# Two reorderings on VectorE around the seven-product multiplications of a fused two-layer attention kernel

## The chip, the cores and the metric

The kernel runs on one core of one Trainium2 chip. The metric is the time of one execution on the device, in microseconds; less is better. A profile of one execution of the kernel before is at hand, with a trace of every instruction of each engine.

## The reference: what is computed

Two layers run over 32 independent batches of 512 nodes with 512 features, in fp32.

```python
# layer 0, eight heads of 64 columns
q, k, v = x @ Wq.T + bq, x @ Wk.T + bk, x @ Wv.T + bv
logits = q @ k.T / sqrt(64) + log(clip(adj, 1e-8))       # per head
out    = softmax(logits) @ v                             # heads joined
y      = layer_norm(x + out @ Wo.T + bo) * gamma + beta
# layer 1
f      = y @ fc_w.T + fc_b
lg     = (f @ q_w.T + q_b) + (f @ k_w.T + k_b).T
m      = lg + (1 - adj) * -1e9
att    = softmax(where(m >= 0, m, 0.01 * m))
result = att @ f + y
```

The log of the adjacency is applied in the kernel as a factor on the exponentials, and layer 1 is computed as `(att @ n) @ fc` plus a residual, where `n` holds the normalised rows before gamma and beta.

## The kernel before, in words

The program is written out by hand: every engine gets its instructions in the order in which the Python code issues them, and a tile framework adds the semaphore waits that the data need. TensorE (PE in the profile) does the matrix products, VectorE (DVE) and ScalarE (ACT) the elementwise work, and the SyncE queue (SP) issues all transfers.

**Slots.** For each batch `b` there are four slots `slot(b, p)`, one for each pair of heads. A slot computes the scores and exponentials of its pair (`score`, lines L849 to L858), multiplies the exponentials by the adjacency (`factors`, L866), and forms the values of the pair before (`values`, L891). Into this are woven the stages of earlier and later batches, so that several batches are in work at once. `factors(b, p, 0)` handles the first two of the four 128x1024 blocks of exponentials, and `factors(b, p, 1)` the other two.

**Products with seven multiplications.** Large products are done by a Strassen-Winograd scheme: seven products of quarters in place of eight, at the price of sums and differences of quarters on VectorE. Every product is 16 matmuls of 128x64 weights by 256 columns, recorded at L213 (the helper `halves`).

**First slot of batch b, for b from 2 to 31 (30 slots).** Besides its own pair it does the following.

- `scale(b - 1, 0)` (L946) multiplies two head outputs by the inverse row sums `R`, and `first_difference` (L954) prepares a quarter for the later output projection. Then comes `factors(b, 0, 0)`.
- `eT(b - 2)` (L572): four transposes in 32x32 blocks of `eP`, the layer-1 attention weights of batch b - 2. Sixteen transfers `eP<-L` have moved the blocks to their places.
- `seven_z(b - 2)`: the product of the normalised rows `n` with those weights. Its quarters are called A (of `n`) and E (of `eP`). `before0` makes `t1 = E12 - E11` (L1048, in a free half of a tile named `R`) and `s1 = A21 + A22` (L1049, in a tile named `third`); `before1` makes A21 = A11 - A21 (L1052); `after0` overwrites E11 and A11 (L1055, L1056). `unit0` runs mul(1), which reads the old A11 and E11, and mul(5), which reads `s1` and `t1`; `unit1` runs mul(6), which reads the new A11 and E11, and mul(2); `unit2` and `unit3` run mul(7), mul(3) and mul(4).
- `scaled(b - 2, ...)` (L464): the residual `yb = n * gamma`, in two halves of 128x1024. `new_yb` takes the buffer `yb`, of which there is one.
- `divided(b - 1, 2)` inverts the sums of the last two pairs of batch b - 1 and sends them through DRAM to `R` (transfers `d<-c`, then `R<-d`).

**Second slot of batch b (b from 1 to 31).** `scale(b - 1, 2)` (L946) waits for that `R`; `first_sum` (L961) adds quarters of the head outputs. Then come `factors(b, 1, 0)` and `sums`, a 128x1024 sum (L876), `factors(b, 1, 1)`, and the output projection `seven_wo` of batch b - 1: mul(1), then mul(5), which reads the result of `first_sum` (matmuls `<-wo_s,oT`), then subtractions of quarters (L770) ahead of its own mul(6).

The order of the work around the change is the order of these calls. The transfers that feed `eP` are issued in the fourth slot of the batch before, after the transfers `R<-d` and eight of the adjacency (`cT`).

Of the kernel before, what the change touches and what calls it, by code (L numbers as in the profile page):

```python
# [30 lines left out]
def kernel(  # L31
# [58 lines left out]
    NC = N // P  # L90
# [4 lines left out]
    KH = DC // 2  # L95
# [114 lines left out]
    def halves(to, left, right, start, stop):  # L210

        for h in range(2):
            nc.tensor.matmul(  # L213
                to[ts(h, DK)], left[:, ts(h, DK)], right,
                start=start, stop=stop, skip_group_check=True,
            )
# [95 lines left out]
    def transpose_units(src, dst, psum, evict, name):  # L312

        units = []
        for i in range(4):
            def unit(i=i):
                pt = psum.tile([P, 512], FP, tag="m", name=f"pt_{name}_{i}")
                for c in range(4):
                    nc.tensor.transpose(pt[:, ts(c, P)], src[:, c, ts(i, P)], ident)
                evict(dst[:, i, :], pt)  # L320
            units.append(unit)
        return units
# [137 lines left out]
    def over(row, cs):  # L460
        return row.unsqueeze(1).to_broadcast([P, cs.stop - cs.start, D])

    def scaled(s, cs):
        nc.vector.tensor_mul(s["yb"][:, cs, :], s["n"][:, cs, :], over(K["gamma"], cs))  # L464
# [39 lines left out]
    def fast(ctx):  # L504
# [8 lines left out]
        S = [dict() for _ in range(B)]  # L513
# [56 lines left out]
        def transposes(dst, src):  # L570
            return [
                lambda c=c: nc.vector.transpose(dst[:, c, :], src[:, c, :]) for c in range(4)  # L572
            ]
# [251 lines left out]
        def long_banks(b):  # L825
            return lambda: [
                lone[i].rearrange("p (n f) -> p n f", n=KH) for i in (2, 0, 1)
            ]
# [32 lines left out]
        def factors(b, p, half):  # L861

            s = S[b]
            for kc in (2 * half, 2 * half + 1):
                at = s["at", p, kc]
                nc.vector.scalar_tensor_tensor(  # L866
                    at, cT[:, kc, :].unsqueeze(1).to_broadcast([P, 2, N]), ADJ_MIN, at,
                    ALU.max, ALU.mult,
                )
# [72 lines left out]
        def scale(b, p):  # L942
            s = S[b]
            for k in range(2):
                oT = s["oT"][p + k]
                nc.vector.tensor_mul(oT, oT, s["R", p][:, k, :])  # L946

        def first_difference(b, to=None):

            s = S[b]  # L950
            oT = s["oT"]
            s["s3"] = to or act.tile([P, KH, H], FP, tag="oT", name=f"s3_{b}", bufs=6)
            for c in range(KH):
                nc.vector.tensor_sub(s["s3"][:, c, :], oT[c][:, :H], oT[c][:, H:])  # L954

        def first_sum(b, to=None):

            oT = S[b]["oT"]
            for c in range(KH):
                into = oT[c][:, H:] if to is None else to[:, c, :]  # L960
                nc.vector.tensor_add(into, oT[c][:, H:], oT[KH + c][:, H:])  # L961
# [39 lines left out]
        def seven_z(b):  # L1001


            s = S[b]
            n, e = s["n"], s["eP"]
            s["zT"] = zT = L1
            s1 = third
            t1 = S[b + 1]["R", 2][:, 1, :].rearrange("p (c n) -> p c n", c=KH)
            A = {f"{i + 1}{j + 1}": n[:, ts(j, KH), ts(i, H)] for i in range(2) for j in range(2)}
            E = {f"{i + 1}{j + 1}": e[:, ts(j, KH), ts(i, H)] for i in range(2) for j in range(2)}  # L1010
            C = {f"{i + 1}{j + 1}": zT[:, ts(i, KH), ts(j, H)] for i in range(2) for j in range(2)}
            left = {1: A["11"], 2: A["12"], 3: A["12"], 4: A["22"], 5: s1, 6: A["11"], 7: A["21"]}
            right = {1: E["11"], 2: E["21"], 3: E["22"], 4: E["21"], 5: t1, 6: E["11"], 7: E["12"]}
            ps = {}
            sub = nc.vector.tensor_sub

            def mul(i, name, first=False):
                for m in range(KH):
                    for t in range(KH):
                        halves(  # L1020
                            ps[name][:, m, :].rearrange("p (c n) -> p c n", c=KH),
                            left[i][:, t, ts(m, P)], right[i][:, :, ts(t, P)],
                            first and m == 0 and t == 0, m == KH - 1 and t == KH - 1,
                        )

            def unit0():
                ps.update(zip("bac", long_banks(f"z{b}")()))
                mul(1, "a", True)
                mul(5, "c", True)
                nc.scalar.copy(ps["b"], ps["a"])  # L1030
                nc.scalar.copy(C["22"], ps["c"])

            def unit1():
                mul(6, "a")
                mul(2, "b")
                nc.scalar.copy(C["12"], ps["a"])
                nc.scalar.copy(C["11"], ps["b"])

            def unit2():
                mul(7, "a")  # L1040
                mul(3, "c")

            def unit3():
                mul(4, "a")
                nc.scalar.copy(C["21"], ps["a"])

            def before0():
                sub(t1, E["12"], E["11"])  # L1048
                nc.vector.tensor_add(s1, A["21"], A["22"])  # L1049

            def before1():
                sub(A["21"], A["11"], A["21"])  # L1052

            def after0():
                sub(E["11"], E["22"], t1)  # L1055
                sub(A["11"], s1, A["11"])  # L1056

            def after1():
                sub(E["12"], E["22"], E["12"])

            def before2():
                sub(A["12"], A["12"], A["11"])
                sub(E["21"], E["21"], E["11"])

            def after2():
                nc.vector.tensor_add(C["22"], ps["a"], C["22"])

            def after3():
                nc.vector.tensor_add(C["12"], ps["c"], C["12"])
            return [unit0, unit1, unit2, unit3], [  # L1070
                before0, before1, after0, after1, before2, after2, after3
            ]

        def eT(b):
            s = S[b]
            if b >= B - 2:
                t = io.tile([P, NC, N], FP, tag="x", name=f"eT_{b}")
                s["eT"] = t.rearrange("p t (c n) -> p t c n", c=NC)
                return transpose_units(s["e"], t, ps_m, nc.scalar.copy, f"e_{b}")
            s["eT"] = s["eP"].rearrange("p c (t n) -> p t c n", t=NC)  # L1080
            return transposes(s["eP"], s["eP"])
# [46 lines left out]
        def new_yb(b):  # L1128
            S[b]["yb"] = act.tile([P, NC, D], FP, tag="yb", name=f"yb_{b}")
# [144 lines left out]
        def run(units):  # L1274
            for u in units:
                u()

        def slot(b, p):
# [20 lines left out]
            if p == 0 and last >= 0:  # L1299
                scale(last, 0)  # L1300
                first_difference(last)
            if p == 1 and last >= 0:
                scale(last, 2)
                first_sum(last)
            factors(b, p, 0)
            fc_sums = right_units(K["fc"], K["fc_s"]) if b == 1 and p == 1 else []
            if p == 1:
                sums(b, p, 0)
# [18 lines left out]
            run(soft[:1])  # L1327
            if p == 0 and last >= 0:
                if b >= 2:
                    run(eT(b - 2))  # L1330
                if b == 1:
                    turn_a((2, 3))
# [6 lines left out]
            else:  # L1339
                next_qk = seven_qk(nxt, 0)  # L1340
            if p == 0 and b >= 2:
                zs, extra = seven_z(b - 2)
                top, bottom = slice(0, KH), slice(KH, NC)
                extra[0]()
                new_yb(b - 2)
                scaled(S[b - 2], top)
                extra[1]()
                run(next_qk[:4])
                zs[0]()
                extra[2]()  # L1350
                run(next_qk[4:])
                extra[3]()
                zs[1]()
                turn_a((2, 3))
                scaled(S[b - 2], bottom)
                extra[4]()
                zs[2]()
                extra[5]()
                divided(last, 2)
                zs[3]()  # L1360
                factors(b, p, 1)
                extra[6]()
                sums(b, p, 0)
            elif p == 0:
                sums(b, p, 0)
                if b == 0:
                    run(first_v[2:3] + next_qk + first_v[3:])
                else:
                    run(next_qk)
                    divided(last, 2)  # L1370
                    spread(ps_o)
# [367 lines left out]
```

## Time and profile before

| what | value |
|---|---|
| median of the runs | 3400.0 us (3398.38 to 3400.63, three runs) |
| the profiled execution | 3400.59 us |
| its span, first to last instruction | 3398.7 us |
| PE matmul busy | 3349.1 us, 99% of the span, 25914 matmuls |
| DVE busy | 3007.2 us, 88% |
| ACT busy | 1394.7 us, 41% |
| transfers | 252.84 MB, queue share of 16 engines 36.1% |
| granted TensorE clock | 1.000 |

The profiled execution has 1.9 us outside the span (3400.59 less 3398.7). "Busy" is time in which an engine has a recorded instruction under way. Matmuls are pipelined: 16 matmuls of one product start 1.73 us apart in all, but the last one is recorded as ending 0.17 us later than the next product may start. Gaps between starts therefore say more than busy time. A wait line of the profile names the waiting instruction, then the one that released it, then the total, the number of times and the longest.

### The profile page before, as it was taken

What the parts mean: (1) busy time and instruction counts of PE and PEld (TensorE: products, weight loads), DVE (VectorE), ACT (ScalarE), POOL (GpSimd) and SP (SyncE); (2) the same over time, 40 slices, a digit from 0 to 9 for tenths busy, and PEclk for the clock granted to TensorE, in tenths of its full rate; (3) what the DMA queues carried; (4) which work ended last, traced back from release to release, by engine and by line L of the source; (5) the groups of instructions that cost most, each with busy time, mean ns of one, the idle gap of its engine ahead of it and who ended that gap; (6) DMA issues with size and microseconds to landing.
All of it is one profiled execution on the core that took longest, in us unless ns stands there. A gap on an engine that the chain in (4) does not pass through costs nothing.

```text
span 3398.7 us, 64226 instructions
## 1 busy us (share of the span) xinstructions
PE 3349.1 (99%) x25914; PEld 1914.6 (56%) x25914; DVE 3007.2 (88%) x5284; ACT 1394.7 (41%) x2501; POOL 0.9 (0%) x9
## 2 busy tenths in 40 slices
PE   9999999999999999999999999999999999999999
PEld 4555555555555555555555555555555555555555
DVE  7888998889998888888898988998889988889888
ACT  3443443334443444434444343443344443444443
POOL 0000000000000000000000000000000000000000
PEclk9999999999999999999999999999999999999999
DMA  5234342343333443333424334343343333343321
GB/s 127 52 63 91 66 85 67 57 91 82 70 74 55 86 90 61 80 65 70 91 60 88 68 59 91 66 86 67 57 91 83 69 75 60 80 90 62 81 71 47
DMA packets 881655, 252.84 MB, mean 74 GB/s; under 512 B 806732, under 2 KB 809036, under 8 KB 881352
## 3 DMA queue, kind: packets, MB, share of 16 engines
q1 hardware_dynamic: 881352, 248.67, 36.1%
q8 instruction: 206, 3.38, 0.4%
q14 instruction: 97, 0.79, 0.1%
HBM read 182.46 MB, written 34.65 MB: 64 GB/s over the span
## 4 chain that ended last, share of the span: by engine, by line
PE 81%; DVE 9%; SPq 5%; DMA 3%; issue 1%; ACT 1%; DVEq 0%; ACTq 0%
PE f L213 17%; PE mx L213 13%; PE my L213 13%; PE mz L213 13%; PE po L891 12%; PE sc L849 9%; SPq L148 3%; DVE eP L572 2%; DMA d<-R 1%; DVE at L866 1%; PE my L849 1%; SPq L542 1%; DVE yb L464 1%; PE mz L849 1%; DMA d<-c 1%
## 5 line engine op out<-in xcount | busy, mean ns | idle before, releaser
L858 ACT ACTIVATE at<-sc 128x1024 f32<-128x1024 f32 x386 | 384.4, 1031 | 751.4 <-PE sc L849 751.4
L866 DVE SCALAR_TENSOR_TENSOR at<-cT,at 128x1024 f32<-128x1024 f32 x512 | 599.9, 1214 | 3.1 <-ACT at L858 3.1
L891 PE MATMUL po<-at,v 128*64 128x512 f32 x2048 | 490.6, 599 | 2.0 <-DVE fold_more L298 1.6
L849 PE MATMUL sc<-qT,kT 64*128 64x512 f32 x1544 | 387.5, 607 | 0.0
L879 DVE TENSOR_TENSOR as<-as,at 128x1024 f32<-128x1024 f32 x254 | 310.3, 1222 | 5.4
L891 PEld LDWEIGHTS po<-at,v 128*64 128x64 f32 x2048 | 138.6, 136 | 268.5 <-issue 247.2
L849 PEld LDWEIGHTS sc<-qT,kT 64*128 64x128 f32 x1544 | 138.3, 186 | 225.2 <-issue 172.0
L213 PE MATMUL f<-xT,wq 128*64 128x256 f32 x2032 | 262.4, 379 | 0.0
L213 PE MATMUL f<-T,qk_s 128*64 128x256 f32 x2032 | 251.6, 379 | 0.6 <-ACT f L651 0.6
L213 PEld LDWEIGHTS f<-xT,wq 128*64 128x64 f32 x2032 | 146.0, 137 | 100.6 <-issue 28.0
L213 PEld LDWEIGHTS f<-T,qk_s 128*64 128x64 f32 x2032 | 145.7, 137 | 74.6 <-ACT f L651 1.4
L946 DVE TENSOR_TENSOR oT<-oT,R 128x512 f32<-128x512 f32 x126 | 80.2, 677 | 96.7 <-DMA R<-d 96.7
L876 DVE TENSOR_TENSOR as<-at,at 128x1024 f32<-128x1024 f32 x128 | 156.0, 1219 | 1.1
L657 ACT ACTIVATE qT<-f,bq 128x256 f32<-128x256 f32 x127 | 60.1, 473 | 231.9 <-PE f L213 231.9
L663 ACT ACTIVATE kT<-f,bk 128x256 f32<-128x256 f32 x127 | 59.8, 471 | 192.2 <-PE f L213 192.2
L213 PE MATMUL f<-T,wk 128*64 128x256 f32 x1016 | 131.2, 379 | 0.0
L213 PE MATMUL f<-xT,wk 128*64 128x256 f32 x1016 | 131.2, 379 | 0.0
L213 PE MATMUL f<-xT,qk_s 128*64 128x256 f32 x1016 | 131.2, 379 | 0.0
L213 PE MATMUL mz<-eP,n 128*64 128x256 f32 x960 | 115.6, 380 | 10.8 <-DVE n L1056 8.1
L213 PE MATMUL mx<-eP,n 128*64 128x256 f32 x960 | 115.6, 380 | 10.4 <-DVE n L1056 9.2
L213 PE MATMUL my<-eP,n 128*64 128x256 f32 x960 | 115.5, 380 | 10.2 <-DVE n L1056 9.1
L572 DVE STREAM_TRANSPOSE eP<-eP 128x512 f32<-128x512 f32 x120 | 74.7, 681 | 48.3 <-DMA d<-R 48.3
(419 smaller groups left out, 6134.5 us busy)
## 6 DMA issues: line engine op xcount, KB each, us to landing
cT<-in_adj_dram SPq DMA_DIRECT2D x512, 64.0 KB
R<-d SPq DMA_DIRECT2D x126, 256.0 KB
x<-in_x_dram SPq DMA_DIRECT2D x124, 256.0 KB
n<-in_x_dram SPq DMA_DIRECT2D x31, 1024.0 KB
L<-in_adj_dram SPq DMA_DIRECT2D x60, 512.0 KB
eP<-L SPq DMA_DIRECT2D x480, 64.0 KB
out_dram<-yb SPq DMA_DIRECT2D x58, 512.0 KB
w<-dk SPq DMA_DIRECT2D x32, 256.0 KB
```

Source lines behind the costliest of these rows:

```text
L148: nc.sync.dma_start(out=dst[j * BL : (j + 1) * BL, :, :].rearrange("r c (t q f) -> q r (c t) f", q=P // BL, f=BL)[i], in_=src[i * BL : (i ...
L213: nc.tensor.matmul(to[ts(h, DK)], left[:, ts(h, DK)], right, start=start, stop=stop, skip_group_check=True,)
L572: lambda c=c: nc.vector.transpose(dst[:, c, :], src[:, c, :]) for c in range(4)
L657: nc.scalar.activation(q[:, H:], ps["a"], AF.Identity, bias=bq)
L663: nc.scalar.activation(k[:, :H], ps["d"], AF.Identity, bias=bk, scale=-1.0)
L849: nc.tensor.matmul(parts[j], s["kT", p][rows, ts(kc, P)], s["qT", p][rows, :], start=True, stop=True,)
L858: nc.scalar.activation(at, sc, AF.Exp, scale=SCALE)
L866: nc.vector.scalar_tensor_tensor(at, cT[:, kc, :].unsqueeze(1).to_broadcast([P, 2, N]), ADJ_MIN, at, ALU.max, ALU.mult,)
L876: nc.vector.tensor_add(s["as", p], s["at", p, 0], s["at", p, 1])
L879: nc.vector.tensor_add(s["as", p], s["as", p], s["at", p, kc])
L891: nc.tensor.matmul(s["po", p][j * DK : (j + 1) * DK, :], s["v"][h // 4][:, kc, ts(h % 4, DK)], s["at", p, kc][:, j, :], start=(kc == 0), s ...
L946: nc.vector.tensor_mul(oT, oT, s["R", p][:, k, :])
```

## The change

In the first slot, for b of 2 and more, the calls `new_yb`, `scaled(top)` and `before0` move ahead of the four transposes `eT`. `before0` keeps only `s1 = A21 + A22`, which needs nothing of `eP`; `t1 = E12 - E11` goes to the head of `before1`, behind the transposes. In the second slot, `factors(b, 1, 0)` moves ahead of `scale(b - 1, 2)` and `first_sum`. In the first slot the order of `scale(b - 1, 0)`, `first_difference` and `factors(b, 0, 0)` stays as it is.

```diff
             def before0():
+                nc.vector.tensor_add(s1, A["21"], A["22"])
+
+            def before1():
                 sub(t1, E["12"], E["11"])
-                nc.vector.tensor_add(s1, A["21"], A["22"])
-
-            def before1():
                 sub(A["21"], A["11"], A["21"])
...
             if p == 0 and last >= 0:
                 scale(last, 0)
                 first_difference(last)
+            factors(b, p, 0)
             if p == 1 and last >= 0:
                 scale(last, 2)
                 first_sum(last)
-            factors(b, p, 0)
...
             if p == 0 and last >= 0:
                 if b >= 2:
+                    new_yb(b - 2)
+                    scaled(S[b - 2], slice(0, KH))
+                    zs, extra = seven_z(b - 2)
+                    extra[0]()
                     run(eT(b - 2))
...
             if p == 0 and b >= 2:
-                zs, extra = seven_z(b - 2)
-                top, bottom = slice(0, KH), slice(KH, NC)
-                extra[0]()
-                new_yb(b - 2)
-                scaled(S[b - 2], top)
                 extra[1]()
                 run(next_qk[:4])
                 zs[0]()
...
-                scaled(S[b - 2], bottom)
+                scaled(S[b - 2], slice(KH, NC))
```

## The prediction

> **What bounds the kernel now.** I read the page first, then the waits, then the timeline of single slots on VectorE and TensorE side by side. The first page line says that TensorE is the bound:
>
> ```profile
> PE 3349.1 (99%) x25914; PEld 1914.6 (56%) x25914; DVE 3007.2 (88%) x5284; ACT 1394.7 (41%) x2501; POOL 0.9 (0%) x9
> ```
>
> Only what shortens TensorE's row of matmuls, or a gap in it, can move the time. No matmul is removed, so I look for gaps. The waits show one kind that returns in nearly every batch, and two long waits of VectorE:
>
> ```profile
> DVE oT L946 <- DMA R<-d: 96.7, 31, 4.7
> DVE eP L572 <- DMA d<-R: 48.3, 30, 3.6
> PE mx L213 <- DVE n L1056: 9.2, 10, 1.2
> PE my L213 <- DVE n L1056: 9.1, 9, 1.2
> PE mz L213 <- DVE n L1056: 8.1, 8, 1.2
> ```
>
> TensorE waits 27 times for L1056, the new A11 that mul(6) reads. VectorE idles 1.6 us in each of the 30 first slots ahead of the transposes of eP, and 3.1 us in each of the 31 second slots ahead of the scaling (96.7/31). Now the first slot of batch 10. VectorE:
>
> ```profile
> 1031.31 2.35 DVE L866 SCALAR_TENSOR_TENSOR at<-cT,at 128x1024 f32<-128x1024 f32 x2
> 1035.60 2.49 DVE L572 STREAM_TRANSPOSE eP<-eP 128x512 f32<-128x512 f32 x4 [1.94 <-DMA d<-R]
> 1038.13 0.69 DVE L1048 TENSOR_TENSOR R<-eP 128x512 f32<-128x512 f32 x1
> 1038.74 0.68 DVE L1049 TENSOR_TENSOR third<-n 128x512 f32<-128x512 f32 x1
> 1039.34 1.22 DVE L464 TENSOR_TENSOR yb<-n,gamma 128x1024 f32<-128x1024 f32 x1
> 1040.59 0.69 DVE L1052 TENSOR_TENSOR n<-n 128x512 f32<-128x512 f32 x1
> 1041.20 0.69 DVE L1055 TENSOR_TENSOR eP<-eP,R 128x512 f32<-128x512 f32 x1
> 1041.80 0.69 DVE L1056 TENSOR_TENSOR n<-third,n 128x512 f32<-128x512 f32 x1
> ```
>
> and TensorE, mul(1), mul(5), mul(6):
>
> ```profile
> 1037.44 1.90 PE L213 MATMUL my<-eP,n 128*64 128x256 f32 x16
> 1039.47 1.95 PE L213 MATMUL mz<-R,third 128*64 128x256 f32 x16
> 1042.63 1.95 PE L213 MATMUL my<-eP,n 128*64 128x256 f32 x16 [1.21 <-DVE n L1056]
> ```
>
> A product that waits for nothing starts 1.73 us after the one before it. So mul(5) was due at 1039.17 and came 0.30 late, after s1 (end 1039.42); mul(6) was due at 1041.20 and came 1.43 late, 0.15 after A11 was ready (1042.49). Between the transposes and A11 stand s1 (0.60 from start to start) and the upper residual rows (1.25), neither of which reads eP, while VectorE had stood idle 1.94 us just before. This slot lost 1.73 us.
>
> **What the skill says.** The Trainium skill, "VectorE: DVE Perf Modes", section "The TRN2 errata", gives an fp32 tensor_tensor (N + 151)/0.96 ns, which is 691 ns for 512 elements, and another row of 58 + N cycles, 594 ns. The trace shows both: 0.69 recorded, 0.60 from start to start. "TensorE: Matmul & The Clock Gate", section "Architectural detail", calls VectorE's queue strict FIFO; the trace agrees, since the ready s1 stood behind the waiting transposes. "DMA: Bandwidth & Descriptors", section "Anatomy of one DMA", puts some 2.0 us of fixed cost on a transfer: here the queue finished issuing `eP<-L` at 1033.59 (start 1022.52 and 11.07) and the transposes began at 1035.60, 2.0 later. That wait can't be shortened by this change, only filled.
>
> **The change in the first slot.** Nothing is added or removed; every instruction keeps its duration, and no transfer changes its place on the SP queue. Times below count from the due start of mul(1).
>
> - *Where the moved work lands.* The factors end at -3.77 in nearly every batch. The residual rows (1.14 to the start of what follows) and s1 (0.68) then end at about -2.0, and the transposes can start from -2.05. Where eP lands earlier than that (23 of 30 slots), they start later than before, by up to 1.1 us. mul(1) reads the first two transposes and starts 1.36 after their start (seen where it is late), so it would be ready at -0.69: covered by 0.7 us.
> - *mul(5)* needs t1, which ends 3.22 after the start of the transposes, at 1.17; with 0.14 for the semaphore 1.31, due 1.73. Covered by 0.4.
> - *mul(6)* needs A11. Before, A11 ended 6.88 after the start of the transposes; without s1 and the residual rows it is 5.03, so 2.98. But E11 may only be overwritten when mul(1) has read it, at about 1.90, so L1055 starts at 1.95, A11 ends at 3.24, and with 0.15 mul(6) is ready at 3.39, due 3.45. Covered by only 0.06; I take it as no wait.
> - *What is behind it on VectorE:* the additions for q and k, E12, the adjacency transposes, the lower residual rows, A12, E21. They keep their distance to A11 (E21 ends 5.32 later, A12 0.60 before that), so A12 is usable at 8.1, and mul(3) is due at 8.64. Covered by 0.5; before it was 0.5 too.
> - *The yb buffer* is taken some 5 us earlier. The stores that must have left it were issued 40.8 and 34.3 us before mul(1): free.
>
> Reading the starts of mul(1), mul(5), mul(6) in all 30 first slots, the summed lateness is **42.4 us**: 0.4 to 1.8 in 25 slots, and 2.6 to 3.4 in five (batches 2, 6, 13, 20, 27), where eP landed so late that mul(1) itself waited, as in batch 6 with 1.17 us. With the steps above applied to each slot's own landing time, the 25 go to zero and the five keep 0.8 to 1.6: **5.6 us** stay. Gain 36.8 us. Is the landing fixed relative to TensorE? In 24 of 30 slots the transfers `R<-d` that open this row on SP start 22.5 us before mul(1), within 0.03, and SP then issues eight `cT` and sixteen `eP` back to back; so the row hangs on the slot's own work and moves with it, and its scatter (3 us) will be drawn anew.
>
> **The change in the second slot**, shown for batch 10:
>
> ```profile
> 1057.58 1.29 DVE L946 TENSOR_TENSOR oT<-oT,R 128x512 f32<-128x512 f32 x2 [4.21 <-DMA R<-d]
> 1058.79 0.75 DVE L961 TENSOR_TENSOR oT<-oT,oT 128x256 f32<-128x256 f32 x2
> 1059.46 2.35 DVE L866 SCALAR_TENSOR_TENSOR at<-cT,at 128x1024 f32<-128x1024 f32 x2
> ```
>
> ```profile
> 1060.26 1.90 PE L213 MATMUL mz<-wo_s,oT 128*64 128x256 f32 x16
> ...
> 1065.73 1.95 PE L213 MATMUL my<-wo_s,oT 128*64 128x256 f32 x16
> ```
>
> The second `wo_s,oT` product was due 6.91 after the first product of the projection and waited for L770, which stands behind the factors: 0.29 late. Over 31 slots this happened in four (batches 3, 10, 22, 29), 2.0 us in all. With the two factors (2.28 us) in the idle time ahead of the scaling, L770 ends up to 2.28 earlier, and the 2.0 go. The price: the factors need the exponentials, which end 3.20 and 2.29 before the projection's first product in every slot, so they run until -0.88. Scaling and first sum (1.96) then end at 1.08 where R came early (before: -0.8 to 0). mul(5) reads that sum and is due at 1.73; the trace has first sums ending as late as 1.34 (batch 22) with no wait. Covered by 0.5.
>
> **Sum.** 42.4 - 5.6 + 2.0 = 38.8 us off the profiled execution of 3400.6, which gives 3361.8. The median of the runs is 0.6 lower, so I say **3362**. A difference of 0.2% (7 us) is about the least that a measurement of this kernel can tell from no change.
>
> **The rivals.**
>
> - *A hold on mul(6) that hides below A11.* mul(6) was never seen earlier than 3.85 after mul(1) (batch 8). Its weights also wait on ScalarE; the waits even name L1031 (36 us), but in batch 8 mul(6) started 0.4 us before L1031 ended, so that is not needed. If something unseen held it at 3.85, the 25 slots would keep 0.4 each: 10 us, giving 3372. A gain beyond the sum needs earlier landings: at most the 5.6, giving 3356.
> - *No change: the landing of eP is bound by the queue, not by the slot.* Then a shorter batch only makes mul(1) wait for eP, and the time stays near 3400. Against it: the fixed 22.5 us above, and transfers at 36.1% of the engines. A landing 1 us later relative to mul(1) would leave 18.6 instead of 5.6, giving 3375.
> - *Slower: the factors ahead of the scaling hold up the output projection.* Place: first sum to mul(5) in 31 second slots. It costs nothing until the sum is 0.5 us later than worked out, then one for one. It outweighs the gain from 38.8/31 = 1.25 beyond that, so 1.75 us later than worked out; at 2.2 the time is 3400 + 31 x 1.7 - 38.8 = 3414. Against it: the exponentials' ends repeat to 0.01 us.
> - *The edits do nothing* because the waits in the way are others: then 3400; the three L1056 lines speak against it.
>
> **How the numbers follow.** My case with its scatter: 86% (3355 to 3368, likeliest 3362). The hidden hold or somewhat later landings: 7% (3368 to 3380). No change: 3%. Slower: 4%. The range of 3355 to 3373 takes in the hidden hold of 3372 and the earlier landings of 3356. Faster by over 0.2%: 0.93; within 0.2%: 0.03; slower: 0.04.
>
> **What would show it.** The waits of PE for L1056 fall from 27 to a few; the idle time before L572 falls from 48.3 to some 8 us, all of it in slots where eP lands late. In the second slot VectorE now waits some 2 us for the exponentials (L866 <- ACT L858, about 60 us in 31 slots), and its wait for R before L946 falls from 96.7 to a few us. "PE <- oT L770" vanishes. Wrong would be mul(6) still late in most first slots with A11 ready, a new PE wait for L961 or L946 in the second slot, or more PE waits for L572 than five or six.

## The result, and the profile after

The changed kernel takes **3361.07 us** (median of four runs, 3359.49 to 3363.72) against 3399.4 us before (four runs): 38.3 us less, ratio 0.9888 with the 95% interval 0.9871 to 0.9905. The profiled execution took 3363.72 us with a span of 3361.9, which is 36.8 below the span before. A later comparison ran both kernels again: 3360.97 us for the changed kernel, but 3392.86 for the kernel before, so a gain of 31.9 us. The time of the changed kernel repeats; that of the kernel before is the one that differs.

TensorE and the chain that ended last, on the page of the changed kernel:

```profile
PE 3343.2 (99%) x25914; PEld 1886.9 (56%) x25914; DVE 3004.2 (89%) x5284; ACT 1394.7 (41%) x2501; POOL 0.9 (0%) x9
...
PE 94%; DVE 2%; SPq 2%; DMA 1%; ACT 1%; issue 0%; DVEq 0%; ACTq 0%
```

Each engine has as many instructions as before. What changed is the chain: TensorE's share of it was 81% before, with 9% for VectorE and 5% for the SP queue. The other engines and the queue now make up 6% of it.

The waits after. First VectorE's, then TensorE's (engine and line, what it waited for, total, times, longest):

```profile
DVE at L866 <- ACT at L858: 67.0, 33, 4.0
...
DVE eP L572 <- DMA d<-R: 8.3, 6, 1.9
...
DVE oT L946 <- DMA R<-d: 0.5, 2, 0.3
```

```profile
PE mx L213 <- DVE eP L572: 1.3, 2, 0.9
PE mz L213 <- DMA c<-d: 1.1, 1, 1.1
PE mz L213 <- DVE eP L572: 0.9, 1, 0.9
...
PE my L213 <- DVE eP L572: 0.5, 1, 0.5
```

No wait of TensorE for L1056 is left, of 27. The five waits in these lines are the mul(1) of the five late slots; the one put down to `c<-d` is that of batch 6, where the transposes of eP were late as in the others. The wait ahead of these transposes fell from 48.3 to 8.3 us and sits in six slots. (The profile names `d<-R` as what ended it. That transfer is issued right behind `eP<-L`; in each of the six slots the transposes began 2.0 us after the last issue of `eP<-L`, as in the slot of the prediction.) The wait for R fell from 96.7 to 0.5 us, but 64 us of it came back as waiting for the exponentials (L866, 3.1 us before): idle time that was moved, not won. The first slot of batch 10, VectorE's timeline and then TensorE's mul(1), mul(5), mul(6):

```profile
1022.33 2.35 DVE L866 SCALAR_TENSOR_TENSOR at<-cT,at 128x1024 f32<-128x1024 f32 x2
1024.60 1.22 DVE L464 TENSOR_TENSOR yb<-n,gamma 128x1024 f32<-128x1024 f32 x1
1025.73 0.69 DVE L1048 TENSOR_TENSOR third<-n 128x512 f32<-128x512 f32 x1
1026.34 2.49 DVE L572 STREAM_TRANSPOSE eP<-eP 128x512 f32<-128x512 f32 x4
1028.87 0.69 DVE L1051 TENSOR_TENSOR R<-eP 128x512 f32<-128x512 f32 x1
1029.48 0.69 DVE L1052 TENSOR_TENSOR n<-n 128x512 f32<-128x512 f32 x1
1030.39 0.69 DVE L1055 TENSOR_TENSOR eP<-eP,R 128x512 f32<-128x512 f32 x1 [0.23 <-PE my L213]
1031.00 0.69 DVE L1056 TENSOR_TENSOR n<-third,n 128x512 f32<-128x512 f32 x1
```

```profile
1028.45 1.90 PE L213 MATMUL my<-eP,n 128*64 128x256 f32 x16
1030.17 1.90 PE L213 MATMUL mz<-R,third 128*64 128x256 f32 x16
1031.90 1.90 PE L213 MATMUL my<-eP,n 128*64 128x256 f32 x16
```

The residual rows and s1 fill the stretch in which VectorE had stood idle, and the transposes follow without a gap. A11 ends at 1031.69 (1031.00 and 0.69). The three products start 1.73 us apart: nothing is late. L1055 now waits 0.23 us for mul(1) to finish reading E11, as worked out.

The lateness of a slot is the time by which mul(1), mul(5) and mul(6) start later than 1.73 us after the product ahead, summed. Read from the starts in all 30 first slots, and from the mul(6) behind L770 in the 31 second slots:

| trace | late in first slots | late behind L770 |
|---|---|---|
| before | 42.2 us | 2.0 us |
| after | 6.4 us | 0.0 us |

(The prediction had read 42.4 for the first number.) The lateness fell by 37.8 us, the span by 36.8. Three small things stand between these numbers. The first of these mul(1) started at 199.3 us in place of 197.7, so 1.6 us were lost ahead of it, where this change does nothing; another 0.8 us were lost near the end of the program. On the other side, a product that had to wait also runs a little slower: from its first to its sixteenth start a late mul(6) takes 1.57 us in place of 1.52, 1.2 us over the 30 slots, which the lateness does not count.

### The profile page after: what moved, and what is told of

Same layout as the page of the kernel before. It is cut to its first block, busy times and chain, and to the rows that moved or that the text cites. A ratio compares the mean times of both kernels' runs of the same rounds, so it can differ in the third digit from the quotient of the medians.

```text
span 3361.9 us, 64316 instructions
## 1 busy us (share of the span) xinstructions
PE 3343.2 (99%) x25914; PEld 1886.9 (56%) x25914; DVE 3004.2 (89%) x5284; ACT 1394.7 (41%) x2501; POOL 0.9 (0%) x9
## 4 chain that ended last, share of the span: by engine, by line
PE 94%; DVE 2%; SPq 2%; DMA 1%; ACT 1%; issue 0%; DVEq 0%; ACTq 0%
PE f L213 21%; PE my L213 15%; PE mx L213 14%; PE mz L213 14%; PE po L891 13%; PE sc L849 10%; SPq L148 1%; PE my L849 1%; PE mz L849 1%; PE mx L849 1%; DVE at L866 1%; PE my L908 1%; PE mx L908 1%; PE mz L908 1%; SPq L542 1%
## 5 line engine op out<-in xcount | busy, mean ns | idle before, releaser
L866 DVE SCALAR_TENSOR_TENSOR at<-cT,at 128x1024 f32<-128x1024 f32 x512 | 600.2, 1215 | 67.0 <-ACT at L858 67.0
L899 ACT COPY oT<-po 128x512 f32<-128x512 f32 x128 | 74.9, 585 | 71.9 <-PE po L891 71.9
L435 ACT ACTIVATE w<-w,q 128x512 f32<-128x512 f32 x128 | 85.3, 716 | 32.9 <-DVE top L436 24.9
```

What stands on the lines that cost most here:

```text
L435: nc.scalar.activation(qk, s["kb"], AF.Identity, bias=s["q"][:, c : c + 1])
L866: nc.vector.scalar_tensor_tensor(at, cT[:, kc, :].unsqueeze(1).to_broadcast([P, 2, N]), ADJ_MIN, at, ALU.max, ALU.mult,)
L899: nc.scalar.copy(s["oT"][p], s["po", p])
```

## Experiments

### Which slot carries the gain

The first-slot edit alone (the second slot as before):

```diff
-            factors(b, p, 0)
             if p == 1 and last >= 0:
                 scale(last, 2)
                 first_sum(last)
+            factors(b, p, 0)
```

> The first-slot edit alone; the second slot keeps the order of the kernel before. My theory (the gain is mul(6) no longer late in the first slots): the summed lateness of mul(1), mul(5), mul(6) falls from 42.4 us to about 6.6, and the 2.0 us of lateness behind L770 stay, so 35.8 us off 3399.4, 3363.6. Rival (the second-slot edit carries a large part, since it cuts the long wait for R of 96.7 us): 3375 or more.

Measured: 3361.56 us against 3395.68, 34.1 us less (ratio 0.9900, 0.9884 to 0.9917). The lateness in its trace is 3.2 us in the first slots and 0.5 behind L770.

The second-slot edit alone, on the kernel before:

```diff
+            factors(b, p, 0)
             if p == 1 and last >= 0:
                 scale(last, 2)
                 first_sum(last)
-            factors(b, p, 0)
```

> The second-slot edit alone; the first slot as before. My theory: only the four late products behind L770 go, 2.0 us, so 3397.4; the wait of VectorE for R all but vanishes from the waits although hardly any time is won, and PE still waits for L1056 some 27 times. Rival (the filled idle time is worth what it lasts, 2.28 us in 31 slots): about 3330 to 3380.

Measured: 3395.18 us against 3395.68, ratio 1.0000 (0.9991 to 1.0009): no difference that can be measured, and certainly not 15 to 65 us. Its waits:

```profile
DVE oT L946 <- DMA R<-d: 0.8, 1, 0.8
```

```profile
PE mx L213 <- DVE n L1056: 10.7, 10, 1.2
PE my L213 <- DVE n L1056: 9.4, 9, 1.2
PE mz L213 <- DVE n L1056: 5.8, 7, 1.2
```

The largest DMA wait of VectorE in the whole kernel, 96.7 us, is gone, and the time stands still, because TensorE still waits 26 times for L1056 (27 before). The gain is the first slot's. The 2.0 us that I gave the second slot lie inside the interval and were neither shown nor refuted by the times. The traces show them: in six traces without the edit the lateness behind L770 is 0.5 to 2.1 us, and in the five with it, leaving out a kernel further below that holds this slot up, it is at most 0.1.

### What each moved instruction is worth

The upper residual rows alone ahead of the transposes (against the kernel before):

```diff
                 if b >= 2:
+                    new_yb(b - 2)
+                    scaled(S[b - 2], slice(0, KH))
                     run(eT(b - 2))
...
                 extra[0]()
-                new_yb(b - 2)
-                scaled(S[b - 2], top)
```

> Of the first-slot edit only the upper residual rows (1.25 us) move ahead of the transposes; s1 stays between them and A11, and the second slot is as before. My theory (a gain is capped by what each slot was late, slot by slot): lateness 42.4 to 10.7, so 31.7 off 3399.4, 3367.7. Rival (the gain is shared by duration, 1.25 of 1.85 of 35.8): 24.2 off, 3375.2.

Measured: 3366.57 us against 3395.68, 29.1 us less (0.9915, 0.9899 to 0.9932); lateness 8.2 us.

s1 alone ahead of the transposes, with the residual rows between t1 and A21 (against the changed kernel; the second slot is as in the kernel before):

```diff
             def before1():
                 sub(t1, E["12"], E["11"])
+                new_yb(b)
+                scaled(s, slice(0, KH))
                 sub(A["21"], A["11"], A["21"])
...
                 if b >= 2:
-                    new_yb(b - 2)
-                    scaled(S[b - 2], slice(0, KH))
                     zs, extra = seven_z(b - 2)
                     extra[0]()
```

> Of the first-slot edit only s1 (0.60 us) moves ahead of the transposes; the upper residual rows stay between t1 and A21, and the second slot is as before. My theory (capped slot by slot): lateness 42.4 to 25.0, so 17.4 off 3399.4, 3382.0; with the rows alone that makes 49.1, more than both together. Rival (shared by duration, 0.60 of 1.85 of 35.8): 11.6 off, 3387.8.

Measured: 3377.62 us against 3395.68, 18.1 us less (0.9952, 0.9935 to 0.9968); lateness 18.6 us.

Alone the two are worth 29.1 and 18.1, together 34.1 in the same comparison. Each slot can give back only what it was late, so the second move finds most slots already on time. The gains sit close to the forecasts of 31.7 and 17.4. Shares by duration (24.2 and 11.6) would just fit the intervals of the times, but not the traces: they would leave some 18 and 31 us of lateness, and 8.2 and 18.6 are left. Shares would also add up to the 34.1 of both together, and the two gains add up to 47.2. That the gains fit so well is in part luck. The lateness left was forecast at 10.7 and 25.0, so the kernels came out faster than forecast (3366.57 against 3367.7, 3377.62 against 3382.0), and the kernel before was faster in this comparison too. The runs of the three kernels do not overlap: at most 3362.32 with both moved, 3366.16 to 3367.41 with the rows, at least 3376.46 with s1.

### Was the slower case ruled out for the right reason?

The second slot's 1.14 us sum moved ahead of the scaling too:

```diff
             factors(b, p, 0)
+            if p == 1:
+                sums(b, p, 0)
             if p == 1 and last >= 0:
                 scale(last, 2)
                 first_sum(last)
...
             if p == 1:
-                sums(b, p, 0)
                 run(fc_sums[:1])
```

> The changed kernel, and in the second slot the 128x1024 sum of exponentials (1.14 us) also goes ahead of the scaling. It tests the cover of 0.5 us by which I ruled out the slower case. My theory: the first sums end at 2.2 in place of 1.07 after the projection's first product, mul(5) is due at 1.73, so it is late by 0.4 to 0.65 us in each of 31 slots, 12 to 20 us slower than the changed kernel. Rival (mul(5) needs the first sums later than I think, as when their second half is used only by its later matmuls): no more than 5 us slower.

Measured: 3375.14 us (a single run) against 3360.97 for the changed kernel beside it, 14.2 us slower. TensorE's waits of this kernel:

```profile
PE my L213 <- DVE oT L961: 2.7, 11, 0.2
PE mx L213 <- DVE oT L961: 2.4, 10, 0.2
PE mz L213 <- DVE oT L961: 2.4, 10, 0.2
```

All 31 second slots now wait for the first sum. By the starts, mul(5) comes 2.14 after mul(1) in place of 1.73, so 0.41 x 31 = 12.7 us; another 1.2 us is lateness in the first slots, above that of the changed kernel's trace beside it. Batch 10, the first sum and mul(5):

```profile
1053.17 0.75 DVE L961 TENSOR_TENSOR oT<-oT,oT 128x256 f32<-128x256 f32 x2
1053.74 1.95 PE L213 MATMUL mz<-wo_s,oT 128*64 128x256 f32 x16 [0.24 <-DVE oT L961]
```

The first sum is a pair of instructions of 0.42 us each. The pair ends at 1053.92, yet mul(5) starts at 1053.74, 0.15 after the first of the two. So mul(5) needs only the first of them at its start, which is the mechanism that the rival named (though not its size, 5 us at most), and the forecast of 12 to 20 us was met at its lower end. This makes the cover wider than the 0.5 us of the prediction, which let mul(5) wait for both. In 29 of the 31 second slots of the changed kernel the first one ends 0.73 after mul(1), so mul(5) could start at 0.88 and is due at 1.73: covered by 0.85. Moving the 1.14 us sum ahead shifts that end by 1.26, to 1.99, and 1.26 less 0.85 is the 0.41 measured. For comparison, the second slot of batch 10 in the changed kernel, one of the two that wait for R, VectorE and then mul(5):

```profile
1044.58 2.36 DVE L866 SCALAR_TENSOR_TENSOR at<-cT,at 128x1024 f32<-128x1024 f32 x2 [1.99 <-ACT at L858]
1047.11 1.29 DVE L946 TENSOR_TENSOR oT<-oT,R 128x512 f32<-128x512 f32 x2 [0.17 <-DMA R<-d]
1048.32 0.76 DVE L961 TENSOR_TENSOR oT<-oT,oT 128x256 f32<-128x256 f32 x2
1048.99 1.22 DVE L876 TENSOR_TENSOR as<-at,at 128x1024 f32<-128x1024 f32 x1
```

```profile
1049.48 1.90 PE L213 MATMUL mz<-wo_s,oT 128*64 128x256 f32 x16
```

Here both sums have ended at 1049.08 (1048.32 and 0.76), 0.40 ahead of mul(5).

### Where the remaining late slots come from

The five slots in which eP lands late (batches 2, 6, 13, 20, 27) are the same in the two traces. The SP queue ahead of batch 6, changed kernel:

```profile
589.33 0.35 SPq L934 DMA_DIRECT2D d<-c  x1
592.31 1.30 SPq L937 DMA_DIRECT2D R<-d  x2
593.67 5.25 SPq L542 DMA_DIRECT2D cT<-in_adj_dram  x8
599.02 12.11 SPq L148 DMA_DIRECT2D eP<-L  x16
```

The loads `R<-d` read what the store `d<-c` writes, so the queue waits for it; all 24 transfers behind wait along. The Trainium skill, "DMA: Bandwidth & Descriptors", section "Anatomy of one DMA", says that "any semaphore wait happens on the issuing sequencer before dispatch". The section describes transfers issued by GpSimd; the trace agrees for this SyncE queue, which issues nothing between the store and the loads of R. From issue to issue the store takes 1.44 us as a rule, 2.98 here. (Batch 2 is late for another reason: its store takes 1.44, but is issued 22.0 us before mul(1) is due, where the others are issued 23.9 before. Why was not looked for.)

Two ways to test that: take the wait out of the queue's way, or move what makes the store slow. First the changed kernel again, as their base:

> The changed kernel once more, as the base for the two kernels beside it. 0.989 of the kernel before; five late landings of eP at the same batches (2, 6, 13, 20, 27) as in the two traces so far if they belong to the program, at other batches if they are chance.

Measured: 3360.97 us against 3392.86 (0.9907, 0.9890 to 0.9923). mul(1) was late at batches 2, 6 and 27; at 13 and 20 the same stores were slow, and the landing just came in time for mul(1), while the later products still lost 0.2 and 0.3 us.

The adjacency loads between the store and the loads of R:

```diff
-        def divided(b, p):
+        def divided(b, p, between=None):
...
             nc.sync.dma_start(out=d1, in_=c[:, 0, :])
             d1 = d1.rearrange("(k j a) m -> j k (a m)", k=2, j=2)
+            if between:
+                between()
             for j in range(2):
...
             if p == 3 and last >= 0:
-                divided(b, 0)
+                divided(b, 0, lambda: load_a(nxt, (2, 3)))
...
             if p == 3:
-                load_a(nxt, (2, 3))
+                if last < 0:
+                    load_a(nxt, (2, 3))
```

> The changed kernel, and in the fourth slot the eight adjacency loads cT stand on the SP queue between the store d<-c and the loads R<-d, where the queue otherwise stands still for 1.4 us (3 us in nine slots) until the store has landed. My theory (the late landings of eP come from that standstill, which holds every transfer behind it): mul(1) is late in no slot but batch 2, lateness 6.6 to about 1, so 5 to 6 us below the changed kernel. Rival (the landing is bound by the softmax that feeds eP, or by the transfers themselves): the same time as the changed kernel, and the same late batches.

Measured: **3354.97 us** (3354.62 to 3355.98) against 3360.97 (3359.97 to 3362.16) for the changed kernel in the same comparison, 6.0 us less; against the kernel before 0.9888 (0.9872 to 0.9905). The same stretch of its SP queue:

```profile
588.19 0.35 SPq L934 DMA_DIRECT2D d<-c  x1
588.59 5.15 SPq L542 DMA_DIRECT2D cT<-in_adj_dram  x8
593.78 1.30 SPq L939 DMA_DIRECT2D R<-d  x2
595.18 11.66 SPq L148 DMA_DIRECT2D eP<-L  x16
```

The store lands while the adjacency loads are being issued, the standstill is gone, and the last issue of eP comes 1.6 us earlier in the mean (6.0 in place of 4.4 ahead of mul(1)). No first slot is late, not even batch 2's. This version beats both kernels.

Then the fetches of instructions. In the first traces of the kernel before and of the changed one, nine stores `d<-c` took 2.7 to 3.4 us; four of them stand ahead of the batches 6, 13, 20 and 27. In every one of the nine a 16 KB packet of the instruction kind (queue q8) began 0.3 to 1.2 us after the store's issue. Among the 51 that took at most 1.7 us none had a packet beginning in that stretch. Of the other three, two took 1.8 to 1.9 us and the last one of the program 4.8, behind two stores of the output, all without such a packet. The test puts 32 matrix instructions more at the start of the changed kernel, so that the packets fall elsewhere in the work:

```diff
             pt.append(ps_o.tile([P, N], FP, tag="po", name="pt_x_3"))
+            for _ in range(32):
+                nc.tensor.transpose(pt[0][:, :P], ident, ident)
```

> The changed kernel with 32 extra transposes of a constant on TensorE at the very start, while it waits for its first data; nothing else changes, and their result is overwritten. They move each 16 KB block of TensorE's instructions[...] by 64 instructions against the work. My theory (a store d<-c is slow when the fetch of such a block starts 0.3 to 1.2 us after it is issued): from the fetch times of the changed kernel's trace, only 1 of the 62 stores falls on a fetch in place of 9, so eP is late in none of batches 6, 13, 20 and 27, and the time is some 4 us less. Rival (the slow stores go with something counted on the SP queue or in DRAM): the same nine slow stores at the same batches, the same time.

Measured: 3360.88 us, the same as 3360.97. So the forecast time was wrong, and the number of slow stores too: seven, not one. But they are seven other stores, each again with such a packet 0.4 to 1.0 us after its issue, and mul(1) is late at batches 2, 3, 10 and 17; at 6, 13, 20 and 27 it is on time. The store ahead of batch 10, in the shifted kernel and in the changed one:

```profile
1004.71 0.35 SPq L936 DMA_DIRECT2D d<-c  x1
1007.66 1.30 SPq L939 DMA_DIRECT2D R<-d  x2
```

```profile
1004.54 0.35 SPq L934 DMA_DIRECT2D d<-c  x1
1005.99 1.30 SPq L937 DMA_DIRECT2D R<-d  x2
```

Nothing on SP, in DRAM or in the stores was touched, so the slow stores do go with TensorE's instruction stream; the rival, which kept them in place, falls. How the packet delays the store was not measured. Why the count failed was not tested; the stretch is only about 1 us wide, and the packets had to be placed from another kernel's trace.

### The same fault cured from the other side

> The kernel before, for a trace on the chip of the comparison. It tests why the gain differs between sittings (38 us, then 34 and 32). My theory: the kernel before pays one for one for every tenth of a us by which eP lands later, the changed kernel hardly; the other kernels' traces of the second sitting put the last issue of eP 0.1 to 0.2 us earlier, so lateness in the first slots should be 36 to 39 in place of 42.2, and the time falls with it. Rival (the chip differs in something else): lateness 42 at the shorter time.

Measured: 3399.23 us; profiled span 3396.5 us with 39.7 us of lateness, against 3398.7 and 42.2 in the first trace. Landing 0.1 us earlier in the mean goes with 2.5 us less lateness, the direction expected; but the forecast of 36 to 39 was missed, and the runs of this comparison were near 3400 us and not near 3394, so the kernel before at its shorter time was not traced. Why it took 3393 to 3396 in two comparisons stays open. They ran on other chips than this one (4 and 0, here 9), so the chip itself is a rival to an earlier landing, and neither was shown.

> The kernel before with the adjacency loads between the store d<-c and the loads R<-d, and nothing of the change: eP lands some 1.6 us earlier instead of its wait being filled. My theory (the two are two cures of one fault): lateness in the first slots falls from about 38 to 7, some 30 us below the kernel before of this sitting. Rival (what counts is that s1 and the residual rows no longer stand between the transposes and A11): little gain, under 8 us.

Its edit is that of the adjacency loads above, on the kernel before. Measured: 3362.16 us against 3400.32, 38.2 us less (0.9890, 0.9873 to 0.9906); lateness in the first slots 3.2 us. One move on the SP queue is worth about as much as the whole change on VectorE. My theory holds, and the gain was larger than the 30 us forecast: lateness fell from 39.7 to 3.2, where 38 to 7 had been worked out. The fault was that eP landed too late for the work standing behind it on VectorE; either that work is moved ahead of the wait, or the wait is shortened. Together they give only 6 us more than the change alone.

## Why the prediction was right, point by point

- **What bounds the kernel:** TensorE, with gaps in the first slots. Right: 42.2 of 44.2 us of lateness were there, and the first-slot edit alone gives 34.1 us.
- **mul(1) and mul(5) covered:** right. In 25 of the 30 slots both start when due. Where eP is there in time, the transposes start at -2.12, where -2.05 was expected.
- **mul(6) covered by only 0.06:** right to the hundredth. A11 ends 3.24 after mul(1) and mul(6) starts at 3.45, in 24 of 30 slots. Nothing unseen held it at 3.85, so the first rival falls by the trace of the change itself.
- **What stays:** 6.4 us against 5.6 forecast, in the five slots named and a trace in batch 21.
- **"Its scatter will be drawn anew":** wrong for what matters. The five late slots are not drawn. Four of them go with where the fetches of TensorE's instructions fall, and batch 2 is late in every trace of the changed kernel. The rest of the scatter did no harm, being covered, but for 0.1 us in batch 21 of the first trace.
- **The second slot:** the wait moved as forecast (67.0 us for the exponentials, about 60 expected), L770's lateness went, no new wait for L961 came. Its worth of 2.0 us is right in this pair of traces; alone it was too small to measure. One term was mis-sized: mul(5) is covered by 0.85 us and not by 0.5, because it starts on the first of the two sums.
- **The sum:** 38.8 forecast, 37.8 found by starts, 36.8 by spans, 38.3 by medians. The term that was least safe is the lateness before: 39.7 to 42.5 us in the three traces with neither the first-slot edit nor the move on the queue. That the forecast of 3362 came within 1 us is in part luck: the four runs spread over 4.2 us, the profiled one took 3363.72 where 3361.8 was forecast for it, and in the later comparison the gain was 31.9.
- **Rivals:** no change (landing bound by the queue) is refuted by the time, though the queue does delay the landing in four of the five slots. Slower is refuted: no second slot waits for the first sum, and the test that exceeds the cover of 0.85 us pays 14 us.

## What to carry to other kernels

An in-order engine that waits for a transfer should first be given all work behind the wait that doesn't need it; what this brings is not the idle time filled but the lateness of the engine that bounds the kernel, added up slot by slot and capped at each slot's own. A long wait on a covered engine can vanish without a trace in the time (96.7 us here). Before filling a wait, look at why the transfer is late: a queue that waits for one store's landing holds everything issued after it, and work that needs no wait fits into that stretch.

## What the hardware showed that I had not expected

A store of 8 KB to DRAM takes 1.44 us from its issue to the issue of the load that waits for it, but 2.4 to 3.6 us over ten traces when a 16 KB packet of instructions starts 0.3 to 1.2 us after its issue; with a packet 1.2 to 1.5 us after, both occur. Which stores are hit repeats: the same nine are slow in all nine traces without the shift, with a tenth in one of them. 32 extra matrix instructions at the start moved the slow stores to other batches.
